# Two-layer graph attention on one core: another table of order for layer 1's middle groups

## The chip, the core and the metric

The kernel runs on one core of a Trainium2 chip. A core has five engines that each work through their own list of instructions in order: TensorE (PE, matrix products), VectorE (DVE), ScalarE (ACT), GpSimd (POOL) and SyncE (SP, which here only issues DMAs). Sixteen DMA engines move data between DRAM and the on-chip memory. The metric is the device time of one execution in microseconds (us), the median of several runs; less is better.

## The reference

128 graphs of 128 nodes with 512 features pass two attention layers, both in fp32. Each has eight heads of 64 columns, and a graph's adjacency weights its attention.

```python
# layer 0
Q, K, V = x @ W_q + b_q, x @ W_k + b_k, x @ W_v + b_v          # 8 heads of 64
scores = Q K^T / 8 + a[:, :, None] + c[:, None, :] + b_g + log(adj + 1e-9)
x = softmax(scores) V + x                                       # a, c = x @ w_g halves
# layer 1
q, k, v = x @ Wq.T + bq, x @ Wk.T + bk, x @ Wv.T + bv
logits = q k^T / 8 + log(clip(adj, 1e-8))
out = (softmax(logits) v) @ Wo.T + bo
return layer_norm(x + out) * gamma + beta
```

## The kernel before, in words

**Groups.** Four graphs make a group, so each layer has 32 groups: t = 0 to 31 are layer 0, t = 32 to 63 layer 1. One group's four graphs are multiplied with a weight together, and the 512x512 weights are cut twice by a Strassen scheme: POOL forms sums of the inputs (`outer_sums`, `inner_sums`), PE multiplies them with sums of weights, and DVE and ACT combine the products (`inner`, `matrix`). Layer 0 has three such products a group (v, q, k), layer 1 four (v, q, k and the output product o).

**Attention of a group.** `begin_attention` does the scores of graphs 2 and 3, and `end_attention`, recorded with the next group, does the rest: `mix` (weights times v on PE, a reciprocal and a multiplication on DVE, giving tile `o`) for graphs 2 and 3, the scores of graphs 0 and 1, and their `mix`. The weights E of a group lie in the buffer of its own input `xT`, so the input of the group after next can be loaded into a half of that buffer only when the `mix` that reads the half is done.

**The round trip of o.** In layer 1 the output product wants `o` turned. The turn is done through DRAM: `store_blocks` (line 611) writes each pair of graphs with four DMAs of 128 KB in blocks of 32 x 32 (pieces of 128 bytes), `load_mixed` (line 886) reads them back with one DMA of 512 KB into `gw`, and two transposes on DVE (`turn`, line 645) turn the blocks inside. Then POOL forms the sums of `gw`, and PE starts the o product. Each layer 1 group makes two such round trips: first for graphs 2 and 3, then for graphs 0 and 1.

**The rest of layer 1.** `residual` (line 892) adds the layer's input to the o product with an accumulating DMA that POOL issues (tile `h`, 512 KB, two a group). `norm_and_store` (line 920) takes row statistics on DVE (`bn_stats`), a root on ACT and POOL, scales on ACT, multiplies by gamma and adds beta on POOL, and stores the result with one DMA of 512 KB a pair (`out_dram<-h`), issued by SP.

**What sets the order.** Every operation is first only recorded by the class `Plan` (line 379), with the operations that it depends on. `tabled` (line 490) gives each operation a time from a written table and `issue` (line 517) emits them all in the order of these times (an operation never comes before one that it depends on). So a table holds nothing but an order: an engine's list is the operations of that engine sorted by their times. The tables are `PATTERNS`, `FIRST`, `CHANGE` and `LAST` (lines 97 to 376). A row of `PATTERNS` holds a first and a last group, a start, a period and one number for each operation of a group, in the order of recording and in hundredths of a us; operation j of group t gets

```python
key += [start + period * (group - 1 - first) + v / 100 for v in at]
```

The first row orders groups 3 to 29 (layer 0, 293 operations each), the second groups 36 to 60 (layer 1, 360 operations each). `FIRST`, `CHANGE` and `LAST` give single times to the operations of groups 0 to 2, 30 to 35, and 61 to the end. A group's numbers span about three periods, so operations of three groups are interleaved at any time.

**Names used below.** "Offset" is an operation's number in the second row, in us. Offsets that differ by a whole period stand at the same place of the repeating order.

Of the kernel before, what the change touches and what calls it, by code (L numbers as in the profile page):

```python
# [42 lines left out]
class Strassen:  # L43
# [40 lines left out]
    def inner_weight(t, x, i):  # L84
# [13 lines left out]
    (3, 29, 75.15, 41.905, [int(v) for v in '''  # L98
# [15 lines left out]
    (36, 60, 1510.52, 52.967, [int(v) for v in '''  # L114
        0 2930 860 496 2847 3286 541 3411 3609 3788 4077 3130 3268 4711 3342 4821 4931 5206 5110 4780 4890 5000 5561
        3847 3993 4012 3727 3850 3932 4276 4148 4084 4212 4099 4436 4697 4335 4448 5174 5445 5464 4595 5089 5132
        5600 5664 5728 5536 11578 12485 15772 3944 4055 4173 4537 4693 4816 4868 5001 5087 5133 5295 5360 5491 5535
        5625 4145 4551 4619 4737 4824 4893 4999 5068 5152 5199 5797 5929 5972 6016 6084 5271 5404 5472 5533 5579
        5647 5710 5778 5885 5931 5598 5666 5734 5761 5841 5992 6060 6136 6191 6237 6308 6144 6213 6281 6308 6388
        6456 6519 6587 6650 6696 5392 5448 5516 5550 5622 5691 5754 5822 5907 5953 6032 6103 6256 6300 6475 6543  # L120
        6589 6004 6147 6215 6242 6344 6412 6562 6631 6715 6762 6672 6781 6934 6978 7046 7092 6381 6431 6500 6526
        6606 6674 6737 6823 6869 6915 7009 7065 7165 7192 7240 7308 7393 7461 7546 7593 7663 7138 7196 7277 7304
        7349 7418 7502 7571 7787 7834 6769 6825 6893 6975 7022 7098 7153 7221 7284 7330 7380 7459 7568 7655 7699
        7767 7813 6835 6890 6959 6992 7109 7190 7306 7374 7437 7483 7897 7941 8094 8181 8249 8295 7556 7612 7680
        7707 7744 7812 7853 7921 8028 8074 7736 7809 7878 7934 7984 8053 8137 8206 8268 8343 8425 8341 8389 8525
        8552 8717 8786 8892 8974 9122 9168 8505 8843 8995 8742 8855 4719 6013 6074 6172 7037 6976 7223 7545 6157
        7738 7120 7476 8234 7669 8496 9939 9746 10338 6316 7421 9333 9043 7907 8050 8118 8145 8225 8293 8334 8404
        8476 8522 8805 8849 8980 9308 9451 8162 8290 8369 8395 8432 8501 8761 8829 9286 9369 9651 9695 9739 9804
        9872 8497 8936 9109 9183 9242 9430 9607 9676 9782 9933 10006 10077 10146 10179 10252 10321 10405 10556 10635
        10681 10822 9945 10034 10102 10163 10209 10277 10340 10408 10569 10616 10698 12140 12478 12416 12539 12559  # L130
        12663 12644 12759 12780 13283 13600 12880 13159 13407 13731 10904 13021 13782 13239 13432 13866 14241 14128
        14326 14348 14505 14795 14422 14919 15112 15243
# [3 lines left out]
        9176 14164 1989 1188 3627 0 45 90 135 45 0 180 90 270 135 360 315 405 0 501 576 551 906 721 796 771 846 950  # L136
        450 225 559 995 1040 860 905 1341 1277 1687 796 1514 4006 7717 15960 3671 22491 16218 16005 1266 1396 1648
        2107 1857 1987 2409 2775 2895 3025 3145 3886 1022 1249 1373 1497 2372 2504 1824 1955 2836 2967 2044 2175
        3166 3452 2496 2628 3647 4087 2712 3514 4159 941 985 1160 1203 1516 1597 1641 1684 1728 1796 1028 1072 1116
        1422 1587 1903 1947 1991 2034 2227 1466 1509 1553 1816 2349 2515 2559 2603 2646 2715 2340 2384 2428 2471  # L140
        2540 935 981 3418 1208 681 2003 4073 3501 2249 3331 4908 3377 2168 2960 5637 6398 2290 4032 4702 5940 1247
        1291 1334 1378 1446 2018 2165 2209 2253 2297 2787 2833 1772 1859 2078 2122 2288 2909 2996 3084 3127 3195
        3241 2952 3040 3258 3346 3414 3521 3608 3652 3696 3764 3390 3433 3477 3564 3633 1146 2331 3290 5280 1948
        2661 4620 5115 3001 6022 6316 6068 1621 3083 7138 6357 6604 6686 7396 7437 2690 2821 2865 3302 3370 3416
        3739 3783 3827 3914 3982 4028 2734 2777 3171 3215 3693 4089 4133 4177 4220 4288 4334 3870 3958 4264 4308
        4382 4483 4723 4789 4832 4901 4439 4570 4679 5007 5075 2620 3125 5679 5981 5321 6439 6522 6563 4661 5362
        5720 6274 3042 8397 8438 8479 3459 5761 8521 6109 5138 5375 5571 5476 5751 1450 1149 1815 1085 3265 2199
        1386 1751 1879 3475 2071 495 668 1943 3536 2135 1213 1578 604 3825 2007 2263 732 3607 4765 9474 3562 5156
        3907 4114 4743 4243 3558 3771 4372 4441 4510 5444 5871 5802 4578 4867 4949 5403 4991 5234 5156 5577 5513
        6682 6150 7311 6766 7172 7767 7899 9052 9844 8859 9394 10025 3794 4045 4174 4200 4395 4464 4526 4595 4657  # L150
        4704 4876 4920 4963 5051 5136 3766 4002 4070 4217 4351 4443 4614 4682 4767 4826 5438 5525 5635 5678 5897
        4899 5095 5163 5190 5350 5419 5482 5550 5613 5690 4973 5569 5790 5817 5908 5979 6094 6227 6291 6337 6480
        5970 6181 6250 6276 6524 6593 6677 6746 6809 6886 5722 5870 5888 6000 6890 5952 6075 6093 6140 7014 10028
        7935 7762 8775 7890 6312 7022 7255 6581 6767 8131 8254 8273 8512 8600 6918 8263 8319 8647 8735 9476 8901
        9596 9473 8837 13511 11456 13512 5207 5394 5639 5666 5864 5958 6138 6206 6269 6315 6361 6590 6634 6765 6831
        6899 6986 5763 5820 5889 5916 6050 6118 6225 6459 6568 6615 7104 7213 7301 7388 7456 7502 6553 6721 6789
        6816 6874 6947 7016 7085 7148 7194 7267 7344 7413 7439 7519 7587 7672 7741 7869 7915 8024 7548 7629 7697
        7724 7782 7850 7935 8003 8066 8112 6959 7060 7128 7155 7257 7374 7432 7500 7563 7609 7655 7738 7825 7978
        8022 8240 8286 6833 7169 7294 7374 7476 7544 7585 7653 7716 7762 8361 8427 8470 8514 8582 8628 7835 7891
        7961 7988 8088 8173 8230 8298 8405 8451 8213 8274 8342 8552 8645 8713 8842 8927 9017 9063 9134 8674 8733  # L160
        8801 8828 8886 9019 9170 9326 9491 9538 9235 9645 9865 9472 9598 3716 5265 3370 3434 6675 5393 3498 5201
        3780 6968 5457 5521 4900 5585 6398 5329 5028 4964 5092 6248 10288 9475 11900 9477 12834 13555 10027 11835
        7478 7643 7891 8015 7179 7253 8328 7327 8145 8983 8218 9203 6481 6645 8287 7602 10861 11386 10613 11323
        11598 12930 12671 13036 13014 13145 13046 13210 13513 13956 13211 13447 14184 8185 8317 8386 8412 8558 8626
        8689 8757 8820 8866 8973 9039 9082 9126 9205 8524 8602 8702 8728 8776 8845 8929 8998 9214 9265 9513 9557
        9600 9688 9756 9366 9447 9573 9600 9644 9717 9775 9844 9884 9885 10056 10125 10194 10220 10257 10326 10367
        10457 10498 10544 10626 10101 10213 10281 10308 10410 10687 10754 10811 10885 11050 10027 10150 10169 10188
        11474 9819 10106 10254 10390 10737 13094 11815 11899 13671 11656 10520 11222 11462 10756 10812 11902 12025
        12044 12156 12603 11125 11685 12034 12090 12178 12837 12967 12968 13029 12966 14175 13514 19145 9617 9732
        9800 9827 9983 10115 10169 10263 10345 10391 10437 10841 10950 10994 11038 11106 11159 9338 9939 10008 10084  # L170
        10301 10369 10454 10605 10732 10778 11311 11377 11464 11508 11576 11664 10857 10907 10975 11002 11082 11123
        11224 11373 11374 11401 10699 10797 11019 11142 11421 11581 11639 11707 11771 11817 11926 11709 11793 11861
        11888 12001 12069 12329 12397 12438 12484 11194 11267 11502 11529 11595 11664 11727 11796 11880 11927 11973
        12110 12154 12197 12285 12353 12399 11474 11552 11620 11647 11684 11752 11835 11905 12044 12331 12460 12525
        12569 12657 12725 12812 12008 12066 12135 12161 12241 12309 12372 12441 12504 12550 12623 12700 12769 12795
        12832 12965 13029 13114 13160 13183 13289 12858 12920 12992 13019 13073 13481 13635 13703 13809 13856 13379
        13790 13938 13615 13728
'''.split()]
# [196 lines left out]
'''.split()]  # L375
REST = FIRST, CHANGE, LAST

# [145 lines left out]
def fast_path(ctx, tc, args, GOOD, bad):  # L523
# [33 lines left out]

    LAST = 2 * NG
    NI = len(Strassen.INSIDE)
# [436 lines left out]
    waiting = None  # L996
    for t in range(LAST):
        nc.mark()
# [345 lines left out]
```

## Time and profile before

| | us |
|---|---|
| three runs | 3161.75, 3161.84, 3162.72 |
| their median | 3161.84 |
| the profiled execution | 3164.67 |
| its span, from the first to the last instruction | 3162.8 |
| PE busy in the span | 3074.8 (97%) |
| DVE, POOL, ACT busy | 2289.2, 2219.9, 1800.1 |

The time of a run lies 1.9 us over the span of the same execution. All instructions that the tables order are issued by line 520, so the profile's rows tell them apart by tile: `gw` is the loaded o of layer 1 (in layer 0 it is a work buffer), `x1d_o` the DRAM tensor between store and load, `xT` a group's input, `bankA`, `bankB` and `bankC` the accumulators of the products, `h` the result of the o product. A window is given in us from the span's start; layer 0 fills the span to about 1350, layer 1 the rest.

### The profile page before, as it was taken

Reading aid. Unit: us, or ns where it says so; the run is one execution under the profiler, and the core shown is the slowest. Engines: PE = TensorE matmul, PEld = TensorE weight load, DVE = VectorE, ACT = ScalarE, POOL = GpSimd, SP = SyncE. Lnnn points to the kernel's source line nnn. Section 1 sums busy time; section 2 is a strip of 40 time slices with the busy share of each in tenths; the row PEclk is TensorE's granted clock in tenths of the full one; section 3 lists DMA queues with packets and bytes.
Section 4 is the critical chain, followed back from the end, with each engine's and each line's share of the span. In section 5 each row is a group of like instructions: output and inputs, shape, how many; then the busy total and the mean of one; then the engine's idle time right before and its main releaser. Section 6 shows DMA issues by size and latency. Waiting matters only on the chain.

```text
span 3162.8 us, 121314 instructions
## 1 busy us (share of the span) xinstructions
PE 3074.8 (97%) x50394; PEld 2685.3 (85%) x50394; DVE 2289.2 (72%) x5066; ACT 1800.1 (57%) x5183; POOL 2219.9 (70%) x2679
## 2 busy tenths in 40 slices
PE   9999999999999999999999999999999999999997
PEld 7888888888888888878888888888888888888886
DVE  6777777777777777757767677677776767777777
ACT  4666666666666666635555555555555555555554
POOL 8666766666666676696768577676767758677686
PEclk9999999999999999999999999999999999999999
DMA  5665555555555555633444535345353443534444
GB/s 115 129 124 122 112 111 116 108 119 116 112 122 117 116 111 113 144 99 92 110 97 98 116 79 114 93 99 115 85 119 88 98 109 85 128 79 113 94 100 107
DMA packets 963099, 341.88 MB, mean 108 GB/s; under 512 B 864240, under 2 KB 871408, under 8 KB 962544
## 3 DMA queue, kind: packets, MB, share of 16 engines
q1 hardware_dynamic: 944416, 299.74, 41.2%
q0 software_dynamic: 16864, 32.51, 6.2%
q8 instruction: 397, 6.50, 0.8%
q10 hardware_dynamic: 1264, 1.84, 0.2%
q14 instruction: 158, 1.29, 0.1%
HBM read 192.42 MB, written 141.56 MB: 106 GB/s over the span
## 4 chain that ended last, share of the span: by engine, by line
PE 78%; DMA 8%; DVE 4%; SPq 4%; POOL 3%; issue 2%; ACT 1%; ACTq 0%; DVEq 0%; POOLq 0%
PE bankA L520 37%; PE s L520 14%; PE bankB L520 14%; PE bankC L520 13%; SPq L520 4%; DMA x1d_o<-o 4%; DMA gw<-x1d_o 3%; DVE h L520 1%; POOL T L520 1%; POOL w L520 1%; POOL wi L520 1%; DVE xT L520 1%; DVE gw L520 1%; ACT h L520 0%; DVE o L520 0%
## 5 line engine op out<-in xcount | busy, mean ns | idle before, releaser
L520 PE MATMUL bankA<-T,w 128*64 128x256 f32 (+1 forms) x4232 | 541.0, 354 | 0.7 <-ACT bankA L520 0.7
L520 DVE TENSOR_TENSOR bankA<-bankA,s 128x128 f32<-128x128 f32 x868 | 254.2, 296 | 272.1 <-PE bankA L520 181.2
L520 DVE TENSOR_TENSOR bankC<-bankC,s 128x128 f32<-128x128 f32 x652 | 193.5, 297 | 170.1 <-PE bankC L520 74.7
L520 PEld LDWEIGHTS bankA<-T,w 128*64 128x64 f32 x4232 | 277.7, 138 | 40.6 <-ACT bankA L520 0.9
L520 DVE TENSOR_TENSOR bankB<-bankB,s 128x128 f32<-128x128 f32 x650 | 190.4, 293 | 142.1 <-PE bankB L520 122.2
L520 POOL TENSOR_TENSOR gw<-w,gw 128x512 f32<-128x512 f32 x128 | 164.7, 1293 | 165.6 <-ACT gw L520 115.4
L520 POOL TENSOR_TENSOR gw<-xn,gw 128x512 f32<-128x512 f32 x128 | 162.9, 1278 | 158.2 <-ACT gw L520 100.6
L520 PE MATMUL bankA<-w,T 128*64 128x256 f32 (+1 forms) x2116 | 265.0, 352 | 0.0
L520 PEld LDWEIGHTS s<-qT,kT 64*128 64x128 f32 x4096 | 238.6, 188 | 29.3 <-issue 20.1
L520 PE MATMUL s<-qT,kT 64*128 64x128 f32 x4096 | 263.1, 278 | 0.2 <-DVE kT L520 0.2
L520 ACT ACTIVATE bankA<-ident 128x256 f32<-128x256 f32 x434 | 167.9, 387 | 166.5 <-DVE v L520 64.8
L520 PE MATMUL bankC<-xT,w 128*64 128x128 f32 (+1 forms) x2296 | 231.5, 281 | 0.1
L520 ACT ACTIVATE gw<-gw 128x512 f32<-128x512 f32 x256 | 161.7, 632 | 113.6 <-POOL gw L520 113.3
L520 POOL TENSOR_TENSOR innerB<-gw 128x256 f32<-128x256 f32 x31 | 22.6, 730 | 257.7 <-DVE gw L520 252.4
L520 ACT ACTIVATE bankC<-ident 128x256 f32<-128x256 f32 x326 | 125.0, 383 | 119.5 <-DVE h L520 42.3
L520 ACT COPY s<-bankA 128x128 f32<-128x128 f32 x434 | 114.3, 263 | 128.6 <-PE bankA L520 124.0
L520 DVE STREAM_TRANSPOSE xT<-xT 128x512 f32<-128x512 f32 x252 | 175.1, 697 | 3.9 <-DMA xT<-x1d_b 3.9
L520 ACT ACTIVATE bankB<-ident 128x256 f32<-128x256 f32 x325 | 125.5, 386 | 82.8 <-DVE u L520 27.9
L520 ACT ACTIVATE s<-s,c 128x1024 f32<-128x1024 f32 x128 | 139.6, 1091 | 51.5 <-PE s L520 51.3
L520 PE MATMUL bankA<-w,xn 128*64 128x256 f32 x1364 | 168.3, 350 | 0.0
L520 ACT ACTIVATE s<-s 128x1024 f32<-128x1024 f32 x128 | 124.0, 1006 | 77.3 <-PE s L520 77.3
L520 PEld LDWEIGHTS bankC<-xT,w 128*64 128x64 f32 x2296 | 143.6, 138 | 24.9 <-ACT bankC L520 16.9
(257 smaller groups left out, 10110.6 us busy)
## 6 DMA issues: line engine op xcount, KB each, us to landing
xT<-x1d_b SPq DMA_DIRECT2D x64, 512.0 KB, 4.7
xT<-in_x_dram SPq DMA_DIRECT2D x496, 64.0 KB, 3.5
x1d_o<-o SPq DMA_DIRECT2D x248, 128.0 KB, 4.8
gw<-x1d_o SPq DMA_DIRECT2D x62, 512.0 KB, 4.3
h<-x1d_n POOLq DMA_DIRECT2D x62, 512.0 KB, 7.3
out_dram<-h SPq DMA_DIRECT2D x60, 512.0 KB, 3.0
xn<-in_x_dram SPq DMA_DIRECT2D x32, 512.0 KB, 4.7
x1d_b<-w SPq DMA_DIRECT2D x128, 128.0 KB, 3.7
```

Of the source, the lines that this page charges most:

```text
L520: self.tc.keep_in_program_order(getattr(getattr(self.nc, engine), method)(*args, **kw))
```

## The change

Only numbers change: no operation, no buffer, no DMA and no line of code outside the tables. The row for layer 0 keeps its numbers and starts at 74.64 in place of 75.15. The row for groups 36 to 60 is replaced by that of an earlier kernel, with a period of 53.283 in place of 52.967. `FIRST`, `CHANGE` and `LAST` are replaced throughout. The last entry of all is 2830.01 + 235.91 = 3065.92 before and 2839.45 + 235.49 = 3074.94 after.

```diff
 PATTERNS = (
-    (3, 29, 75.15, 41.905, [int(v) for v in '''
+    (3, 29, 74.64, 41.905, [int(v) for v in '''
...
-    (36, 60, 1510.52, 52.967, [int(v) for v in '''
-        0 2930 860 496 2847 3286 541 3411 3609 3788 4077 3130 3268 4711 3342 4821 4931 5206 5110 4780 4890 5000 5561
...
+    (36, 60, 1507.38, 53.283, [int(v) for v in '''
+        636 2132 2744 0 1336 1664 45 3910 4158 5246 4668 3258 4406 4929 4998 5067 5177 5940 5416 3217 3869 5375 5136
...
-CHANGE = 16.42, [int(v) for v in '''
+CHANGE = 21.35, [int(v) for v in '''
...
-LAST = 2830.01, [int(v) for v in '''
+LAST = 2839.45, [int(v) for v in '''
```

The offsets of the operations that the prediction speaks of (the index counts a row's numbers from 0):

| operation | index | before | after |
|---|---|---|---|
| load of the group's input, graphs 0 and 1 | 0 | 0.00 | 6.36 |
| load of the group's input, graphs 2 and 3 | 3 | 4.96 | 0.00 |
| load of the adjacency | 6 | 5.41 | 0.45 |
| turns of the input | 2, 4, 1, 5 | 8.60, 28.47, 29.30, 32.86 | 27.44, 13.36, 21.32, 16.64 |
| four stores of o, graphs 2 and 3 | 31, 30, 32, 29 | 40.84, 41.48, 42.12, 42.76 | 44.25, 46.62, 44.89, 45.53 |
| load of o, graphs 2 and 3 | 245 | 47.19 | 52.83 |
| its two turns | 246, 247 | 60.13, 60.74 | 60.95, 59.64 |
| mix of graphs 1 and 0 on PE | 41, 38 | 45.95, 51.74 | 50.20, 55.35 |
| four stores of o, graphs 0 and 1 | 47, 44, 45, 46 | 55.36, 56.00, 56.64, 57.28 | 60.73, 61.37, 60.09, 59.00 |
| load of o, graphs 0 and 1 | 248 | 61.72 | 67.58 |
| its two turns | 250, 249 | 69.76, 70.37 | 79.29, 80.11 |
| DVE's addition behind them in the order before | 181 | 70.98 | 74.39 |
| POOL's first sum of the loaded o | 255 | 71.20 | 80.94 |
| first o product on PE | 268 | 80.50 | 85.89 |
| accumulating loads of h | 328, 344 | 106.98, 109.04 | 109.48, 111.08 |
| first row statistics of each pair | 329 and 345, or 331 and 345 | 121.40, 130.21 | 120.54, 126.45 |
| result stores, graphs 0 and 1, graphs 2 and 3 | 343, 359 | 137.31, 152.43 | 132.22, 152.74 |
| POOL's last addition ahead of the second of them | 358, or 355 | 151.12 | 151.31 |

## The prediction

> **What bounds the kernel now.** I read the page first, then busy time by stretches, then the waits of layer 1's middle groups, then one group engine by engine.
>
> The page: PE is busy 97% of the span, but the chain that ended last also runs through DMA and SP's queue, so PE is not waited for all the time.
>
> ```profile
> PE 3074.8 (97%) x50394; PEld 2685.3 (85%) x50394; DVE 2289.2 (72%) x5066; ACT 1800.1 (57%) x5183; POOL 2219.9 (70%) x2679
> ...
> PE 78%; DMA 8%; DVE 4%; SPq 4%; POOL 3%; issue 2%; ACT 1%; ACTq 0%; DVEq 0%; POOLq 0%
> ```
>
> Busy time by stretches: layer 0's middle, the middle of layer 1 (24 groups, 36 to 60), the end.
>
> ```profile
> core 0: us, PE busy (x) PEld busy (x) DVE busy (x) ACT busy (x) POOL busy (x), PEclk, DMA share, GB/s
> 200.00:1250.00 1050.00, 1048.66 (x17720) 917.03 (x17718) 773.03 (x1726) 664.33 (x1953) 706.08 (x775) 1.00 0.56 115
> 1596.00:2940.00 1344.00, 1290.30 (x21128) 1141.28 (x21126) 975.95 (x2184) 731.12 (x2087) 947.26 (x1176) 0.99 0.43 101
> 2940.00:3120.00 180.00, 179.62 (x2958) 158.44 (x2956) 133.79 (x306) 104.33 (x298) 139.97 (x175) 1.00 0.42 102
> ```
>
> Layer 0 and the end leave PE next to no idle time. Layer 1's middle leaves 1344 - 1290.3 = 53.7 us, and there alone the clock dips: ten half-rate intervals, 35.9 us in all by the trace's clock records, which cost half of that, 18. Without both a group takes (1344 - 71.7) / 24 = 53.0 us; it takes 56.0.
>
> The waits in that window, PE's and then DVE's:
>
> ```profile
> PE bankA L520 <- DVE bankA L520: 53.0, 25, 3.5
> ```
>
> ```profile
> DVE gw L520 <- DMA gw<-x1d_o: 55.9, 23, 3.8
> ```
>
> All of PE's idle time is one wait, once a group, on an addition of DVE; DVE stands as long for the load of o. One group on DVE and on PE:
>
> ```profile
> 2262.68 1.30 DVE L520 STREAM_TRANSPOSE gw<-gw 128x512 f32<-128x512 f32 x2 [2.33 <-DMA gw<-x1d_o]
> 2263.90 0.27 DVE L520 TENSOR_TENSOR bankA<-bankA,s 128x128 f32<-128x128 f32 x1
> ```
>
> ```profile
> 2264.22 0.44 PE L520 MATMUL bankA<-xT,wi 128*64 128x128 f32 x4 [2.07 <-DVE bankA L520]
> ```
>
> The addition that PE needs has no tie to o. It stands behind two transposes of `gw` in DVE's list, and they wait. SP's queue in the same group shows why the load is late:
>
> ```profile
> 2243.50 0.34 SPq L520 DMA_DIRECT2D xT<-x1d_b  x1
> 2245.99 8.07 SPq L520 DMA_DIRECT2D x1d_o<-o  x4
> 2254.10 2.79 SPq L520 DMA_DIRECT2D xT<-x1d_b  x1
> 2256.94 0.43 SPq L520 DMA_DIRECT2D adjT<-x1d_a  x1
> 2258.57 0.32 SPq L520 DMA_DIRECT2D gw<-x1d_o  x1
> ```
>
> Four stores take 8.07 us to issue; the table spaces them over 1.92. From the first store to the transpose this group needs 16.69 us (2262.68 - 2245.99). The table leaves 69.76 - 55.36 = **14.40**. Over groups 36 to 60 the trace has 17.0 in the mean, 15.1 to 20.0. The other round trip has 60.13 - 40.84 = 19.29 and its load lands after 10.9 (10.2 to 12.2): no wait.
>
> **How far the table's times may be used.** In groups without a stall, POOL and DVE start at most 0.3 us later than their offsets, counted from PE's lateness, and layer 0's 41.905 is run in 41.92. Only SP's stores and what follows them are off. So I take the table's distances, and add what DMAs add.
>
> **The change, part by part.** Same instructions, so the 53.0 us of PE work a group stay; only waits can change.
>
> *Period.* 53.283 against 52.967: 0.316 more, 24 x 0.316 = 7.6 us, on PE's path. The last entries differ by 3074.94 - 3065.92 = 9.0, so 1.4 lies in start, change of layers and end.
>
> *Second round trip.* Stores at 59.00 to 61.37, turn at 79.29: **20.29** in place of 14.40. On SP, the input's pair 2, 3 and the adjacency are now issued before the stores (they stood between stores and load of o), and pair 0, 1 goes between the first store and the other three. POOL's accumulating loads of `h`, which share the DMA engines, move from 1.3 to 2.8 us ahead of the first store (106.98 less a period is 54.01, against 55.36; 109.48 less a period is 56.20, against 59.00). Bounds for the trip: 8.58 (planned issue of the load) + 3.25 (its fastest landing) = 11.8; the mean of 17.0 with all of the moved input load on top (4.7 by the page) = 21.7. I take 17.0, the measured trip: 512 KB enter it, 768 KB leave it, and `h` starts earlier. That is 3.3 inside the window, and the worst trip of before, 20.0, still fits. Stall: 0, at the upper end 1.4 a group. Behind the two transposes DVE then has q's last additions, and POOL the sums of o with 85.89 - 80.94 = 5.0 us to the first o product (9.3 before): a late load would now stop PE at both.
>
> *First round trip.* Window 59.64 - 44.25 = 15.39, down from 19.29, and the second result store (512 KB, POOL's last addition ahead of it) is moved between the third and fourth store on SP. Stores landed 6.1 us after the first issue; plus 0.45 for the later fourth and 3.0 for the result store is 9.6, and the load's 4.4 makes 14.0; the table's 8.58 + 4.4 makes 13.0. Margin 1.4 to 2.4: nothing. If it goes, the same DVE list stops PE.
>
> *Statistics.* `h` is wanted 11.1 and 15.4 us after issue (14.4 and 21.2 before); landings were at most 7.0 and 11.8. Hidden, with 3.6 us left; gone, DVE stands as above. POOL's order changes, but its 39.5 us a group leave 13.8 idle; ACT's 30.5 likewise.
>
> *Clock.* A stall of 3.09 us was followed by half rate, one of 2.54 was not:
>
> ```profile
> 2376.66 0.48 PE L520 MATMUL bankA<-xT,wi 128*64 128x128 f32 x2 [3.09 <-DVE bankA L520]
> ```
>
> ```profile
> 2376.10:2379.40 3.30, 2.74 (x26) 2.74 (x28) 1.74 (x7) 0.81 (x3) 2.74 (x4) 0.50 0.00 0
> 2320.00:2323.40 3.40, 3.40 (x60) 3.33 (x62) 2.28 (x10) 1.58 (x6) 3.24 (x6) 1.00 0.02 5
> ```
>
> So the 18 us go with the stalls. The Trainium skill (TensorE: Matmul & The Clock Gate, Part 1) has the array fall to half rate after an idle window of about 3.4 us; the trace's limit is between 2.54 and 3.09, and by the skill's figure only some stalls here would have cost clock, and the gain by its sum would be smaller by up to 18.
>
> *Change of layers.* PE's lateness against the table grows from 2.8 us at group 33 to 12.4 at 36. The second trips of groups 34 and 35 get 13.97 and 12.78 (13.43 and 15.48 before) and needed 16.2 and 17.9: 2.3 and at most 5.1 late, each with up to 1.7 of half clock, 4.3 to 10.8. I take 7, below the middle, since group 35's loads of `h` also start earlier. *End*: the trips of groups 61 to 63 get 18.8, 14.1, 13.6 and needed 15.1, 15.1, 13.1: about 1 late, with 1 more for the rest: 2. *Start* and layer 0: same order in the middle, other transitions that no row prices; 2.8 as before, between none of it and twice it.
>
> **Sum.** Span before: 3065.9 (table) + 2.8 + 9.6 + 72.0 (groups 36 to 60) + 1.8 + 10.7 (after PE's last products) = 3162.8. After: 3074.9 + 2.8 + 7 + 24 x 0.17 = 4 + 2 + 10.7 = 3101.4, where 0.17 is the 0.07 of a stall-free group and 0.1 for a rare late load. That is 61.4 less. The profiled execution took 3164.67, 2.83 over the median, so the median should go from 3161.84 to about **3100.4; I say 3101**.
>
> **Rivals.**
> 1. *The stores queue behind the input load.* Three of four stores stand behind 512 KB. The trip becomes 21.7, 1.4 late in 25 groups: +35, 3136. For it: SP's 8 us of store issue right behind such a load. Against: there the load of o had two more transfers ahead. The Trainium skill (DMA: Bandwidth & Descriptors, Queues, rings and completion order) says that each DMA engine takes a queue's descriptors in ring order, which speaks for this rival; the trace agrees in so far as these stores land after 5.7 to 9.9 us (medians), and those of the first trip after 2.8 to 3.8.
> 2. *SP waits for POOL inside the first trip* (slower). The fourth store stands behind the result store, the result store behind POOL's addition, planned to end 0.17 us before it. If POOL is X late, X - 1.4 is lost in each of 25 groups; from X = 1.4 + 61.4 / 25 = 3.9 the change loses. At X = 4.1: 2.7 x 25 = 68, 3168; a little more and half clock comes on top. Against: in the window POOL waited 0.9 us in all before its gamma rows.
> 3. *The wait only moves.* Another late operation stops PE as long, and the longer table remains: 3161.8 + 9.0 = 3171. Against: PE had no second wait in 1344 us. If it stops PE by 9 less, there is no change.
>
> **Chances.** Forecast 0.72 (its own range 3092 to 3114: terms above at their ends), rival 1 0.14, rival 2 0.07, rival 3 0.04, no change 0.03. Faster by over 0.2% (about what can be told from no change here) 0.86, within 0.2% 0.03, slower 0.11. The range 3088 to 3140 takes in rival 1.
>
> **What would show it.** Right: the window of 24 groups takes about 1283 us with PE idle under 20 and no half-rate intervals; DVE's wait for `gw` nearly gone; the load of o issued 9 to 13 us after the first store. Wrong: a PE wait on DVE once a group with DVE standing at `gw` or `h`; SP standing for POOL with stores of o behind it; a PE wait of another name. Group 35 should show the largest stall that is left.

## The result and the profile after

The changed kernel takes 3088.5 us (median; 3087.3 to 3089.2), the kernel before 3162.3 beside it: the ratio is 0.9764, with an interval of 0.9747 to 0.9781, so 73.8 us less. The forecast was 3101, with terms that reach from 3092 to 3114 at their ends and a stated range of 3088 to 3140. The median lies below the terms' range, and set against the kernel before in the same rounds (0.9764, where 3088 / 3161.84 is 0.9767) also just under the stated one. In span time the changed kernel has 3085.9 against 3162.8. The totals by engine and the chain that ended last:

```profile
PE 3055.3 (99%) x50394; PEld 2669.2 (86%) x50394; DVE 2277.8 (74%) x5066; ACT 1801.8 (58%) x5183; POOL 2224.6 (72%) x2679
...
PE 97%; DVE 1%; POOL 1%; DMA 1%; issue 0%; ACT 0%; SPq 0%; ACTq 0%; DVEq 0%; POOLq 0%
```

DMA and SP's queue have all but left the chain (1% and 0%, from 8% and 4%); 97% of it is PE's. The stretches are those of before: the change of layers, the 24 groups of layer 1's middle, the end.

```profile
core 0: us, PE busy (x) PEld busy (x) DVE busy (x) ACT busy (x) POOL busy (x), PEclk, DMA share, GB/s
1387.00:1591.38 204.38, 201.27 (x3315) 176.19 (x3312) 146.47 (x325) 106.29 (x307) 149.79 (x213) 1.00 0.46 106
1591.38:2864.14 1272.76, 1268.37 (x21124) 1122.38 (x21120) 966.17 (x2186) 735.70 (x2089) 952.37 (x1177) 1.00 0.45 106
2864.14:3060.00 195.86, 195.48 (x3197) 170.57 (x3194) 143.48 (x324) 107.90 (x305) 148.07 (x181) 1.00 0.43 102
```

The middle takes 1272.76 us where the same 24 groups of before, cut at the same operation, took 1343.29: 70.5 less. PE's idle time there falls from 53.9 to 4.4, the granted clock is 1.00 throughout, and a group takes 1272.76 / 24 = 53.03. All that PE still waits for in these groups is 0.2 us a group:

```profile
PE bankB L520 <- DVE bankB L520: 4.4, 24, 0.2
```

DVE's wait for `gw` from the DMA is no longer in the list of this window. SP's queue around one second round trip, the load of o of the first trip at its head, and DVE's first turn of that group behind it:

```profile
2257.24 0.34 SPq L520 DMA_DIRECT2D gw<-x1d_o  x1
2257.72 0.34 SPq L520 DMA_DIRECT2D xT<-x1d_b  x1
2258.17 0.37 SPq L520 DMA_DIRECT2D adjT<-x1d_a  x1
2264.14 0.58 SPq L520 DMA_DIRECT2D x1d_o<-o  x1
2265.06 0.60 SPq L520 DMA_DIRECT2D xT<-x1d_b  x1
2265.71 7.43 SPq L520 DMA_DIRECT2D x1d_o<-o  x3
2275.97 0.33 SPq L520 DMA_DIRECT2D gw<-x1d_o  x1
...
2284.50 0.70 DVE L520 STREAM_TRANSPOSE gw<-gw 128x512 f32<-128x512 f32 x1
```

The last three stores still occupy SP for 7.43 us, and the load of o is issued 11.83 us after the first store (2275.97 - 2264.14). It is only that nobody stands for it: DVE turns `gw` at 2284.50, 20.4 us after that store.

PE's lateness (how far an operation of PE starts behind its time in the table), read at one operation of each group, says where the time went. Each line is the growth over the stretch; the sum with the table's last entry gives the span.

| us of the span | before | forecast | after |
|---|---|---|---|
| last entry of the table | 3065.9 | 3074.9 | 3074.9 |
| start and layer 0, to group 33 | 2.8 | 2.8 | 6.3 |
| change of layers, 33 to 36 | 9.5 | 7 | 1.9 |
| layer 1's middle, 36 to 60 | 72.1 | 4 | -6.0 |
| end, 60 to the last group | 1.8 | 2 | -0.4 |
| behind PE's last products | 10.7 | 10.7 | 9.2 |
| span | 3162.8 | 3101.4 | 3085.9 |

The theory was that the window of the second round trip, 20.29 for 14.40, is the gain. The experiments ask whether it is, whether it is enough, and what made the four other lines differ. Ratios are to the kernel before in the same rounds on the same chip; that kernel's median lay between 3151 and 3171 from one set of runs to the next, so single times of different sets are not compared. Where an experiment adds lines ahead of it, the code's line 520 is called 522 or 524 in its rows.

### The profile page after: what moved, and what is told of

Its sections match the earlier page's. It is cut to its first block, busy times and chain, and to the rows that moved or that the text cites. A ratio compares the mean times of both kernels' runs of the same rounds, so it can differ in the third digit from the quotient of the medians.

```text
span 3085.9 us, 121031 instructions
## 1 busy us (share of the span) xinstructions
PE 3055.3 (99%) x50394; PEld 2669.2 (86%) x50394; DVE 2277.8 (74%) x5066; ACT 1801.8 (58%) x5183; POOL 2224.6 (72%) x2679
## 4 chain that ended last, share of the span: by engine, by line
PE 97%; DVE 1%; POOL 1%; DMA 1%; issue 0%; ACT 0%; SPq 0%; ACTq 0%; DVEq 0%; POOLq 0%
PE bankA L520 47%; PE bankB L520 17%; PE bankC L520 16%; PE s L520 16%; POOL wi L520 0%; DVE xT L520 0%; DVE bankB L520 0%; DMA x1d_o<-o 0%; DMA w<-in_x_dram 0%; SPq L520 0%; POOL gw L520 0%; POOL w L520 0%; DVE st L520 0%; ACT u L520 0%; DMA gw<-x1d_o 0%
## 5 line engine op out<-in xcount | busy, mean ns | idle before, releaser
L520 PE MATMUL bankA<-T,w 128*64 128x256 f32 (+1 forms) x4232 | 527.2, 351 | 1.4 <-ACT bankA L520 1.4
L520 POOL TENSOR_TENSOR rs<-rs,minus_half 128x2 f32<-128x2 f32 (+1 forms) x66 | 48.2, 732 | 281.1 <-ACT rs L520 281.1
L520 POOL TENSOR_TENSOR h<-h,gamma 128x512 f32<-128x512 f32 x123 | 158.2, 1288 | 36.2 <-ACT h L520 36.0
L520 POOL TENSOR_TENSOR h<-h,beta 128x512 f32<-128x512 f32 x123 | 157.8, 1286 | 2.3
```

What stands on the lines that cost most here:

```text
L520: self.tc.keep_in_program_order(getattr(getattr(self.nc, engine), method)(*args, **kw))
```

## Experiments on the window

**The changed kernel with the two turns put back.** Only DVE's two transposes go ahead in the list, to a window of 14.40 and then of 12.80.

```diff
+for j, v in (250, 7340), (249, 7401):     # window 14.40
+    PATTERNS[1][4][j] = v
...
+for j, v in (250, 7180), (249, 7241):     # window 12.80
+    PATTERNS[1][4][j] = v
```

> The changed kernel, with the two turns of the second load of o moved forward on DVE in groups 36 to 60 (79.29 and 80.11 become 73.40 and 74.01): the window is the 14.40 of before. All else, SP's queue too, is the new order. In the changed kernel's trace the load lands 15.2 us after the first store in the mean (10.9 to 17.3). Theory: what lands after 14.40 is lost, 0.92 us a group, 23 us, plus one half-rate interval (1.7): 3088.5 + 25 = 3113. If the queue's order gave all of the gain: 3088. If it gave nothing and only the window counts, the trip is again 17.0 and the time that of before, 3162.

Measured: 3129.0 us, ratio 0.988 (0.985 to 0.991). PE's wait and DVE's:

```profile
PE bankA L522 <- DVE bankA L522: 31.7, 23, 3.5
```

```profile
DVE gw L522 <- DMA gw<-x1d_o: 14.6, 16, 2.7
```

> As the last, with a window of 12.80 (turns at 71.80 and 72.41). Theory: 2.45 us a group are lost, 61 us, and 7 of 25 groups stand longer than 2.8 us and lose 1.7 more to the half-rate clock: 3088.5 + 73 = 3162, the time of before, with the list of the new order otherwise. Rival A (the new interleaving brings the gain): about 3090 to 3100.

Measured: 3175.7 us, ratio 1.004 (1.002 to 1.005). DVE's wait for the load is 48.2 us here, and PE's largest wait has another name:

```profile
PE bankC L522 <- ACT bankC L522: 55.3, 23, 5.1
```

So the window is a cause: with nothing else touched, 20.3 gives a ratio of 0.976 to 0.980, 14.4 gives 0.988, and 12.8 gives the whole gain back and a little more, while DVE's wait for the load goes from none to 14.6 and 48.2. The wait for the load is not all that the two runs lose: at 14.4 PE stands 31.7 us where DVE stands 14.6, and both came out dearer than the theory's 3113 and 3162, by 14 to 16. At the earlier places the transposes also stand ahead of other operations of DVE; what that costs was not measured apart. At 14.4 the new row still loses less than the old one, which fits its shorter trip (15.2 for 16.9); the second set of experiments is on that.

**The old row with the two turns later.** The reverse: before, only the two transposes moved back, by 5.0 us.

```diff
+for j, v in (250, 7476), (249, 7537):
+    PATTERNS[1][4][j] = v
```

> The order before, with one thing moved: in groups 36 to 60 the two turns of the second load of o go back 5.0 us on DVE (69.76 and 70.37 become 74.76 and 75.37), so the window from the first store to the turn is 19.40 in place of 14.40. Theory (DVE stands at the turn, and with it the addition that PE needs): the load landed 15.1 to 18.1 us after the first store in all these groups but the first (19.9), so nothing is left to wait for; the some 72 us that PE fell behind its table in the middle go, and the time is about 3090, at most 3100. Rival A (the whole new interleaving of PE's and DVE's lists brings the gain, the place of the turns little): above 3150. Rival B (the new order on SP's queue brings it, by a shorter trip through DRAM): above 3150, since that order is as before here.

Measured: 3198.6 us, ratio 1.011 (1.008 to 1.014). The expectation fell. DVE's wait for `gw` was gone, as it should be, but PE now stood for POOL, and longer (62.3 us against 53.0):

```profile
PE bankA L522 <- POOL gw L522: 62.3, 23, 2.7
```

POOL's queue in one group shows why:

```profile
2223.07 0.74 POOL L522 TENSOR_TENSOR innerB<-gw 128x256 f32<-128x256 f32 x1 [2.49 <-DVE gw L522]
...
2228.84 2.53 POOL L522 TENSOR_TENSOR h<-h,gamma 128x512 f32<-128x512 f32 x2
2231.30 1.29 POOL L522 TENSOR_TENSOR h<-h,beta 128x512 f32<-128x512 f32 x1
2232.52 0.76 POOL L522 TENSOR_TENSOR gw<-gw 128x256 f32<-128x256 f32 x1
```

POOL now waits 2.49 us for the turn, and the sum of `gw` that PE needs stands behind three operations on rows of `h`. POOL's list changed with the turn, since an operation never comes before one that it depends on: the small operations on `rs`, the row statistics of `h`, come ahead of the first sum of `gw` in this run (2219.28 and 2223.07 in this group) and came behind it before (2266.48 and 2264.06). The sum that PE needs was then put ahead of the rows:

```diff
-for j, v in (250, 7476), (249, 7537):
+for j, v in (250, 7476), (249, 7537), (257, 7854):
```

> The first try in the old row moved DVE's two transposes 5.0 us later; DVE stopped waiting for the load of o, but PE then waited 2.9 us a group for POOL. The trace puts that on one sum of gw which POOL does behind four rows of h (about 4.9 us of work): it was planned 9.5 us behind the turn and is needed early. Here the same transposes are late and that one sum stands ahead of the four rows of h, so it ends 3.7 us sooner, 0.9 us before PE's product is due. Theory (the old row's loss is only the place of the two turns and of what hangs on them): no stall is left but in the few groups with a trip over 19.4, the group takes 53.0 to 53.2, the whole 3090 to 3100. Rival (the late turn presses on POOL's list as a whole, and the next operation in it takes over the wait): 3150 to 3200.

Measured: 3227.2 us, ratio 1.024 (1.022 to 1.025): the rival. PE's wait became ACT's:

```profile
PE bankB L522 <- ACT bankB L522: 80.3, 23, 3.5
```

**Half the step.** The same two transposes 2.5 us later, a window of 16.9.

> The old row with DVE's two transposes 2.5 us later, a window of 16.9 in place of 14.40; half of the first try, in which POOL stood 2.5 us a group for gw before its sums. Theory (the old row has room for the turn up to where POOL starts its sums, and no more): POOL does not wait, only trips over 16.9 stop PE; by the trips of the kernel before that is 12 us in 25 groups, nearly all without half clock, so the whole falls by 55 to 62, to 3092 to 3100 on a chip where the kernel before takes 3154. Rival (any later turn moves the wait to POOL's list, as the first try and the second did): as the kernel before or slower, 3154 to 3200.

Measured: 3148.3 us, ratio 0.998 (0.996 to 0.999), 7 us less: nearly no gain, the rival again. PE's two waits, then POOL's, ACT's and PE's queue at the same place of one group:

```profile
PE bankC L522 <- ACT bankC L522: 31.7, 22, 1.8
PE bankA L522 <- ACT bankA L522: 14.6, 23, 2.2
```

```profile
2200.57 0.73 POOL L522 TENSOR_TENSOR innerB<-gw 128x256 f32<-128x256 f32 x1 [9.63 <-DVE gw L522]
2201.26 1.27 POOL L522 TENSOR_TENSOR xn<-gw 128x512 f32<-128x512 f32 x1
2202.49 0.72 POOL L522 TENSOR_TENSOR rs<-rs,minus_half 128x2 f32<-128x2 f32 x1
2203.19 0.45 POOL L522 TENSOR_TENSOR inner<-gw,inner 128x128 f32<-128x128 f32 x1
2203.61 0.18 POOL L522 TENSOR_TENSOR rs<-rs 128x2 f32<-128x2 f32 x1
```

```profile
2203.83 0.81 ACT L522 ACTIVATE h<-h,rs 128x512 f32<-128x512 f32 x1 [2.32 <-POOL rs L522]
2204.55 0.36 ACT L522 ACTIVATE bankC<-ident 128x256 f32<-128x256 f32 x1
```

```profile
2204.97 0.44 PE L522 MATMUL bankC<-inner,wi 128*64 128x128 f32 x4 [1.43 <-ACT bankC L522]
```

Here the chain can be read link by link. The row statistics of `h` (`rs`) stand behind POOL's first sums of `gw`, which wait for the turn. ACT's scaling of `h` waits for `rs`, and behind it in ACT's list stands a write to `bankC` that has no tie to `h` but that PE needs. A late turn reaches PE through three in-order lists.

In the changed kernel the statistics are ahead of the turn. Its POOL queue, in the group of SP's queue above:

```profile
2274.85 0.73 POOL L520 TENSOR_TENSOR rs<-rs,minus_half 128x2 f32<-128x2 f32 x1 [9.27 <-ACT rs L520]
...
2276.05 0.20 POOL L520 TENSOR_TENSOR rs<-rs 128x2 f32<-128x2 f32 x1
...
2286.07 0.73 POOL L520 TENSOR_TENSOR innerB<-gw 128x256 f32<-128x256 f32 x1 [0.29 <-DVE gw L520]
```

**Half the step, with the statistics first.** In the old row, DVE's three instructions of the statistics change places with the two turns, and POOL's and ACT's small operations on `rs` go with them, ahead of POOL's first two sums of `gw`.

```diff
+for j, v in ((250, 7226), (249, 7287), (331, 12273), (330, 12335), (332, 12349), (333, 12369),
+             (334, 12473), (335, 12454), (336, 12569), (255, 7370), (251, 7420)):
+    PATTERNS[1][4][j] = v
```

> The old row with the window of 16.9 once more, but with the statistics of h ahead of the turn: DVE's three instructions of the statistics take the place of the two transposes and the transposes theirs, POOL computes rs before its first two sums of gw, ACT's two small operations move with them. In the half step before, DVE turned 2.5 later, POOL's first sum of gw was 2.5 late, rs stood behind it, ACT's scaling of h behind rs, and ACT's write to a bank, which PE needs, behind that: 1.4 us a group, and 0.6 more on ACT behind DVE's late statistics. Theory (the wait moved to the statistics because the old row has them behind the turn; the new row has them ahead of it): these two stalls go, only trips over 16.9 stop PE, 12 us in all: 3090 to 3105 on a chip where the kernel before takes 3154. Rival (some other operation takes over again): 3135 or more.

Measured: 3123.5 us, ratio 0.991 (0.990 to 0.993), between the two expectations. The two waits of 1.4 and 0.6 went, and two shorter ones became visible:

```profile
PE bankA L522 <- POOL gw L522: 13.3, 23, 0.6
PE bankB L522 <- ACT bankB L522: 11.0, 23, 0.5
```

Both lead back to POOL's list, which is 2.4 us late over some 20 us of work: the sum of `gw` behind the rows of `h`, and the second `rs`, behind two sums of the input, with ACT's write to `bankB` behind it.

```diff
+             (257, 8054), (351, 13988), (352, 14188), (350, 14181)
```

> The run with the statistics first, and in it the two places mended that still stopped PE 0.6 us each a group: POOL's last sum of gw goes one row of h forward, and POOL's two small operations for the second rs of h one sum of the input forward each. Theory (the window decides, once the lists behind the turn have no operation in them that comes too late): PE keeps only trips over 16.9 and what the half of a group at the row's end loses; the group takes 53.0 to 53.5 in place of 54.1 and more, the whole 3095 to 3108 where the kernel before takes 3151 to 3156. Rival (POOL's list is 2.4 us late over 20 us of work, so that the next operation takes over): 3115 or more.

Measured: 3110.1 us, ratio 0.983 (0.982 to 0.985). The middle of layer 1, and what PE waits for in it:

```profile
1599.00:2880.00 1281.00, 1272.39 (x21026) 1119.69 (x21022) 971.82 (x2170) 723.21 (x2073) 942.08 (x1169) 1.00 0.45 106
```

```profile
PE bankA L522 <- DVE bankA L522: 3.4, 2, 3.3
PE bankB L522 <- DVE bankB L522: 3.0, 5, 1.6
```

Most groups now take 53.13 to 53.7. PE's lateness grows by 16.2 from group 36 to 60, 5.9 of these in the row's last group, whose second half belongs to `LAST`; by the same reading, at another operation than in the table above, it grew by 70.0 before. The time lies over its expected 3095 to 3108, which were for a kernel before of 3151 to 3156; in these rounds that took 3164.2, and the old change of layers kept its cost (10.4 from group 33 to 36). So with the trip as long as before (16.9) and the old period, the wider window takes away 54 of the 70 us, provided that the operations behind the turn are ordered for it. The window alone, in the old order, takes away next to nothing (7 us in all). The new orders of POOL and ACT with the old window were not run.

## Experiments on the trip

The trip itself, from the first store of o to the landing of the load, became shorter too: 16.9 before, 15.2 after, as means over groups 36 to 60.

**SP's order alone, in the old row.** The input's pair 2, 3 and the adjacency go ahead of the stores, pair 0, 1 between the first store and the rest, as in the changed kernel. The one turn of the input on DVE that this would hold up goes back.

```diff
+for j, v in (3, -50), (6, -45), (0, 250), (2, 2770):
+    PATTERNS[1][4][j] = v
```

> The order before, with SP's queue as in the changed kernel: in groups 36 to 60 the load of the input's graphs 2 and 3 and the adjacency go ahead of the stores of o (4.96 and 5.41 become -0.50 and -0.45), the load of graphs 0 and 1 goes between the first store and the other three (0.00 becomes 2.50), and the one turn on DVE that this load would hold up goes back (8.60 becomes 27.70). The window stays 14.40, and POOL's loads of h stay 1.3 us ahead of the first store. Theory (the trip is shorter because 768 KB no longer lie between the stores and the load of o): landing about 15.2 in place of 16.9, some 0.9 us a group lost in place of 2.6, and fewer half-rate intervals: 3105 to 3125. Rival (three stores stand behind the input load, the first rival of the prediction): landing 2.5 later than before, 3230 or more. Rival (the earlier loads of h shortened the trip, not SP's order): 3162.

Measured: 3176.0 us, ratio 1.002 (1.000 to 1.005), the trip again 16.9. The load of o landed 3.5 us after its issue in place of 4.4, and the last store 0.9 later than before.

**Four runs that moved numbers and no work.** To tell the loads of `h` from the distance of the input load, table times of these were shifted, in both rows:

```diff
+for j in 44, 45, 46, 47, 3, 6, 248:                # before: stores of o 1.9 later
+    PATTERNS[1][4][j] += 190
...
+for j, v in (328, 11093), (344, 11301):            # after: loads of h 1.45 and 1.93 later
+    PATTERNS[1][4][j] = v
...
+for j in 3, 6:                                     # after: input load 2.8 later
+    PATTERNS[1][4][j] += 280
...
+for j, d in (3, 280), (6, 280), (328, 145), (344, 193):   # after: both
+    PATTERNS[1][4][j] += d
```

> The other way round, in the old row: stores of o, and what follows them on SP up to the load of o, 1.9 us later, so that both loads of h stand ahead of the first store; SP's order stays. The window shrinks to 12.5. Theory (the earlier loads of h shorten the trip): trip 15.2 to 16.2 in place of 16.9, so the stall grows by 1 or less a group and the whole is 3160 to 3185 where the kernel before takes 3154. Rival (they do not matter): trip 16.9, stall up by 1.9 a group, 3200 or more.

> The changed kernel with POOL's accumulating loads of h 1.45 and 1.93 us later, so that they stand to the first store of o as in the old row (1.3 ahead of it and 0.7 behind it). The trip is measured from the first store to the load's landing: 16.9 in the kernel before, 15.2 in the changed one; with SP's order alone changed in the old row it stayed at 16.9. Theory (the earlier loads of h shorten the trip): 16.0 to 17.0, the last store landing at 12.4 or later in place of 11.6; the window of 20.3 covers it, and the whole stays at 3088 within 3. Rival (the loads of h do not matter): 15.2 and 11.6.

> The changed kernel with the load of the input's pair 2, 3 and of the adjacency 2.8 us later, so that they are issued 2.9 us ahead of the first store of o in place of 5.7. The loads of h had no part in the length of the trip (two runs), nor had the order on SP alone: where the input stood 2.9 us ahead of the stores in the old row, the load of o landed 0.9 sooner after its issue but the last store 0.9 later. Theory (the trip is shorter because the input's 512 KB are through before the stores start): last store landed at 12.5 to 13.3 in place of 11.6, trip 16.0 to 16.9; the window of 20.3 covers it, the whole 3086 to 3089. Rival (the distance does not matter): 11.6 and 15.2.

> The changed kernel with both moves of which each alone left the trip at 15.0 to 15.1: input pair 2, 3 and adjacency 2.8 us later, loads of h 1.45 and 1.93 later. That is the SP order of the changed kernel with the distances that the run with SP's order alone had in the old row (trip 16.9, last store landed at 13.3). Theory (what shares the DMA engines with the stores counts as a whole; either of the two transfers may run beside them, not both): last store landed at 12.5 or later, trip 16.0 or more. Rival (neither matters, the shorter trip comes from something else in the new row): 11.5 and 15.1. The whole 3085 to 3089 either way.

Measured: 3155.6 us in the first, the kernel before being at 3155.5, with a trip of 16.8; 3086.7, 3085.6 and 3086.3 in the other three, with trips of 15.0 to 15.2. They look like the rivals, and they decide nothing. A table entry gives a place in an engine's list and no time: on SP the lists differ from those of the kernel they came from in five places in the first, none in the second, three in the others, out of some 1550; in the runs with later loads of `h`, each load of the second pair only passes one neighbour on POOL. The trace has the loads of `h` issued 2.62 and 1.07 us ahead of the first store in the second run, and 2.61 and 1.15 in the changed kernel. What the four do show is how well the trip repeats, and that the expectation texts of these runs name distances that were never there.

**Loads of `h` truly later.** Idle additions on POOL ahead of each load, which nothing reads, in the changed kernel.

```diff
         for o in self.tabled():
+            if o.engine == "gpsimd" and o.calls[0][1] == "dma_start":
+                for n in ((96,) * 7, (96,) * 2)[args_name(o)]:
+                    self.tc.keep_in_program_order(self.nc.gpsimd.tensor_tensor(
+                        self.pad[:, :n], self.gamma[:, :n], self.gamma[:, :n], ALU.add))
```

> The changed kernel with idle work on POOL ahead of its accumulating loads of h: seven additions of 128 x 96 ahead of the first, two ahead of the second, into a tile that nothing reads. The runs in which only the table's times of these loads, of the input load or of the stores were moved issued them when they did before, since the table gives an order and no times; they say nothing on the trip. Here the two loads are issued some 1.5 and 2 us later against the first store of o, as in the old row. With SP's order alone changed in the old row, the last store landed at 13.3 and the trip took 16.9; the changed kernel has the same order on SP, loads of h 1.3 and 2.0 earlier, 11.6 and 15.2. Theory (the earlier loads of h are the rest of the difference): last store landed at 12.5 or later, trip 16.0 to 16.9. Rival (they do not matter): 11.6 and 15.2. The window of 20.3 covers both; the whole 3086 to 3095.

Measured: 3101.3 us in one run, over the expected 3086 to 3095, the kernel before at 3171.1 beside it. Worked out from issue and landing of each DMA in the trace, medians over groups 38 to 59, us from the first store of o:

| | loads of h issued | last store landed | load of o issued | landed |
|---|---|---|---|---|
| before | -1.27, 0.87 | 12.25 | 12.42 | 16.61 |
| old row, SP's new order | -1.27, 0.87 | 13.22 | 13.33 | 16.75 |
| changed kernel | -2.61, -1.15 | 11.59 | 11.70 | 15.29 |
| changed kernel, loads of h later | -0.67, 1.54 | 13.72 | 13.81 | 17.27 |

The theory holds in direction and is exceeded in size (it had the trip at 16.0 to 16.9): with SP's order unchanged, loads of `h` 1.9 and 2.7 us later make the last store land 2.1 later and the trip 2.0 longer. Whether the idle additions themselves weigh on the DMAs was not tested apart. Pair 0, 1 amid the stores costs them about a microsecond, the load of o without input ahead of it gains 0.8, and the earlier loads of `h` fit the rest. This run also brings back stalls where windows are narrow. PE's wait for DVE in the change of layers (1387 to 1600), in the changed kernel and here:

```profile
PE bankA L520 <- DVE bankA L520: 2.2, 2, 1.1
```

```profile
PE bankA L524 <- DVE bankA L524: 3.1, 1, 3.1
```

Its lateness grows by 4.9 from group 34 to 35 (1.4 in the changed kernel) and by 8.3 from group 60 to 63 (-0.7). The added work on POOL may have a part in that.

## Experiments on start and change of layers

**The new row alone,** with the old `FIRST`, layer 0 and `CHANGE`. The new row and the new `LAST`, which comes with it, stand 0.42 us earlier than in the changed kernel, to fit.

```diff
-    (36, 60, 1510.52, 52.967, [int(v) for v in '''
+    (36, 60, 1506.96, 53.283, [int(v) for v in '''
...
-LAST = 2830.01, [int(v) for v in '''
+LAST = 2839.03, [int(v) for v in '''
```

> The new row for layer 1's middle groups, with the start, layer 0 and the change of layers of the kernel before, moved 0.4 us so that they fit. Theory (the row is the gain; the new change of layers saves what its own two stalls cost): middle as in the changed kernel, the start 3.5 us cheaper than there, the change of layers dearer by its two stalls in the groups just ahead of the row, 5 to 8: in all 3088 to 3093. Rival (the new row needs the change of layers that was ordered for it, since its first trips start among the old ones): a stall of 3 us or more in several of the first groups, 3100 or more.

Measured: 3093.1 us, ratio 0.981 (0.980 to 0.983); the changed kernel in the same rounds 3088.3, 0.980 (0.978 to 0.981). The change of layers:

```profile
1387.00:1597.00 210.00, 201.84 (x3316) 176.02 (x3313) 147.13 (x329) 108.57 (x311) 144.75 (x205) 1.00 0.44 103
```

PE has 8.2 us idle in it, against 3.1 in the changed kernel's stretch, and its lateness grows by 8.4 from group 33 to 36. So the row, with its end, carries nearly all of the gain, and the new change of layers is worth about 8 less the 3.5 that the new start loses.

**The changed kernel with the old start,** everything behind it 0.51 later.

```diff
-    (3, 29, 74.64, 41.905, [int(v) for v in '''
+    (3, 29, 75.15, 41.905, [int(v) for v in '''
...
-CHANGE = 21.35, [int(v) for v in '''
+CHANGE = 21.86, [int(v) for v in '''
```

> The changed kernel with the old order of the start; everything behind it 0.51 us later in the table, as the start needs. In the changed kernel PE was 4.8 us behind the table after the first groups, in the kernel before 1.5. Theory (that loss belongs to the new order of the start): PE 1.5 behind after group 1, the whole 3.5 - 0.5 = 3.0 us less than the changed kernel, about 3085.5. Rival (the start is bound by its first loads, whatever the order): the same as the changed kernel, plus 0.5.

> The changed kernel once more, on the chip and in the rounds of the others, so that a difference of 3 us can be told: 3088 to 3089.

Measured: 3084.5 us (3083.1 to 3085.5), ratio 0.978 (0.977 to 0.980), the changed kernel 3088.3 (3085.2 to 3089.6). PE is 1.9 behind after group 1 where the changed kernel is 4.7 behind. In the changed kernel the chain that ended last runs through POOL's sums of weights at the start of layer 0:

```profile
18.30 4.66 POOL wi L520 x7
27.90 2.64 POOL wi L520 x4
```

With the old start it does so too (`wi` on POOL has 11.1% of the chain's first 100 us in the changed kernel and 14.9% with the old start), so these rows do not tell what the new start loses; that stays open. The kernel with the old start and everything else new is the fastest of all: 3.8 us under the changed one.

## Why the prediction was right or wrong

- *Second round trip, stall 0.* Right, for the reason given: the load of o lands 10.9 to 17.3 us after the first store, the turn comes at 20.3, and narrowing the window brings the loss back, or more. The length taken, 17.0, was too long; the reason named for a shorter one, that `h` starts earlier, is what the run with later loads of `h` confirms.
- *Period, "7.6 us, on PE's path".* This is the step that failed, and the largest miss: the middle was to cost 24 x 53.283 + 4 = 1282.8 and took 1272.76, 10.0 less. A period is only a spacing of table entries, and the table gives an order. PE's own work, 53.0 us a group, sets the group's time, and the prediction had said so in the sentence before it priced the period. Without the 7.6, and without the 0.1 a group for late loads, its own numbers give 24 x (52.967 + 0.07) = 1272.9.
- *Change of layers, 7.* Measured 1.9. The mechanism was right, the size not: both late trips were priced with a length of 16.2 and 17.9, taken from the old order, and took 15.3 and 14.6. With the loads of `h` held back the stall of group 35 is there again. Group 34 to 35 is still where PE loses most in layer 1 in this profile, 1.4 us; in a second profile of the same kernel the two trips took 13.5 and 13.2, and PE's lateness did not grow there.
- *End, 2.* Measured -0.4, from the same trip length.
- *Start, 2.8.* Measured 6.3. The range given for it, between none and twice 2.8, ended at 5.6. "Other transitions that no row prices" was the honest part; the old start shows 3.8 us for them, and which transition it is stays open.
- *First round trip.* Right: its load landed after 11.7 in the mean and 14.9 at most, of 15.3. Margins of 1.4 to 2.4 were asked for; the worst trip kept 0.4.
- *Statistics and clock.* Right: no wait of DVE for `h` from a DMA, and a clock of 1.00 in the middle. The limit "between 2.54 and 3.09" was read from two stalls and is none: in the same trace a stall of 2.36 us that ends at 1481.15 is followed by half rate from 1481.7. The last section has what decides.
- *Rival 1* (stores behind the input load) is there in size, about a microsecond on the stores, and is more than paid for by the rest. *Rival 2* did not occur. *Rival 3*, the wait that only moves, is what the old row does when the two turns are moved: three orders of it (one with a sum on POOL moved as well) gained 7 and lost 35 and 74 us. The new row escapes it, as the orders that worked in the old row suggest, because its statistics of `h` are ahead of the turn and its POOL list is laid out for it. That the prediction gave the whole gain to the window, and looked behind the turn only for the o product's slack, left out that condition; that the new row meets it was luck for the forecast.

The terms together: start +3.5, change of layers -5.1, middle -10.0, end -2.4, tail -1.5, in all -15.5 against the forecast span of 3101.4. The start's miss hides a part of the others: they come to -19.0.

## What to carry to other kernels

A wait behind a late DMA goes away only if everything that stands behind the waiting instruction, on its own engine and on those that wait for that one, can be late as well; follow those lists link by link before pricing a later place. Where a table gives only an order, its period and its times cost nothing in themselves: price a group by the busiest engine's work, and look at the lists before reading an experiment that moves numbers. Measure a DMA round trip with the traffic of the order it will run in, since what another queue issues a microsecond or two earlier moves it as much as the order on its own queue.

## What was not expected of the hardware

POOL's accumulating loads of `h`, on another queue, weigh on the stores of o as much as anything on SP's own: 1.9 and 2.7 us later, they put 2.1 us on the landing of the last store.

The clock does not answer to a stall's length alone. In the old row with the turns 5.0 later, 23 stalls of PE had 2.71 to 2.75 us. After 18 of them the granted clock fell within the next 3 us, after 5 it did not. Two of them, and the stretch behind each:

```profile
1659.71 0.44 PE L522 MATMUL bankA<-w,gw 128*64 128x128 f32 x4 [2.71 <-POOL gw L522]
...
1832.34 0.44 PE L522 MATMUL bankA<-w,gw 128*64 128x128 f32 x4 [2.73 <-POOL gw L522]
```

```profile
1660.00:1663.20 3.20, 3.20 (x34) 2.87 (x32) 2.26 (x6) 1.04 (x4) 3.12 (x5) 0.52 0.43 163
1832.60:1835.80 3.20, 3.20 (x58) 2.91 (x54) 2.45 (x6) 1.04 (x4) 3.12 (x5) 1.00 0.42 161
```

The same stall is followed by 0.52 in one group and 1.00 in another. What differs is where the stall lies on a fixed grid. By the trace's clock records every half-rate stretch of these groups lasts 3.41 us, and the first ones begin at 1660.13, 1718.16, 1776.19 and 1888.83: their distances are 17, 17 and 33 times 3.413 us. Cut into such steps, each of the 18 stalls puts 2.03 us or more of idle time into one step, and the step behind that one runs at half rate. The 5 others lie across the border of two steps, with at most 1.94 us in either. In the two groups above, PE is busy for 0.70 us of the step from 1656.72 to 1660.13, and for 1.87 us of the step from 1830.80 to 1834.21. From the change of layers up to 3060 us, in all traces of this case, no step falls from full to half rate after less than 1.92 us of idle time in the step before, and none keeps the full rate after more than 1.99 (the ends of matmuls in a trace are modelled). The Trainium skill (TensorE: Matmul & The Clock Gate, Part 1) gives an idle window of about 3.4 us that runs freely. The length and the fixed grid agree with these records; but about 2 us of idle time within a step were enough here, and the measurement decides.
